# Feed-forward down stage: half rows kept in SBUF until their LayerNorm, the second half of the weight lookups split around the PSUM copies

## The chip, the core and the metric

The kernel runs on one NeuronCore of a Trainium2 chip. The metric is the device time of one execution in microseconds (us); lower is better. A core has TensorE (PE, matmuls into PSUM), VectorE (DVE), ScalarE (ACT), GpSimd (POOL) and SyncE (SP, which here issues all DMAs). Each engine works its own queue of instructions in order and waits on semaphores for the others.

## What is computed

One transformer block in float32 over 2048 rows of 1024: attention, and then a feed-forward part whose weights are 4-bit codes. Cut to what matters here:

```python
x = x + layernorm(attention(layernorm(x)))
# dequant(c, s) = NF4[c] * s, one scale per block of 64 inputs
h = layernorm(x)
inter = silu(h @ dequant(gate).T) * (h @ dequant(up).T)   # 2048 x 2752
y = inter @ dequant(down).T                               # 2048 x 1024
out = x + (y - mean(y)) / sqrt(var(y) + 1e-5)             # per row
```

The change lies in the last two lines: the down product and its LayerNorm with the residual.

## The kernel before

The stages follow each other on TensorE: projections and attention, output projection with LayerNorm, gate and up products, and from 2643 us on the down stage.

**Down stage, passes.** The 1024 output columns are taken in two halves (`n`), the 2048 rows in two groups (`g`) of eight tiles of 128 rows. That gives four passes (n, g) = (0,0), (0,1), (1,0), (1,1). In a pass the eight tiles accumulate in all eight PSUM banks, while `kt` runs over the 22 blocks of 128 inner columns (the last has 64). For each `kt`, `down` issues three matmuls per tile (a float32 number is split into two parts, `mm3`, L114 to L116; two matmuls at the last `kt`, L625 and L626). In the last pass alone the final six `kt` (LAST = 6) are held back and done tile by tile, so that the tiles are complete one after the other.

**Activations.** `load_inter` (L613, L616) brings 1 MB of `inter` per `kt` from HBM into a tile `it`, from the slot tag "hd", which has seven buffers of 8 KB per partition.

**Weights.** `down_weights` makes the weights of one (n, kt). `looked_up` loads the codes and scales into a tile `cs` (tag "pw", three buffers, L490 to L492), computes the NF4 value as minima and maxima of straight lines, seven lines `ln` on ACT (L499; tag "t2", three buffers) and ten operations on DVE (L494 to L512), and `split` writes the two parts into `wd` (L120, L121). Two `kt` share a buffer of `wd`, from the tags "pa", "w" and "xc" (13 buffers together, 11 needed for one half). So two pairs of the second half can be made at once, the others as pass (0,1) frees the buffers of the first half. `make(upto)` issues lookups in order until `upto` of the 44 are issued.

**Ends of passes.** With n = 0, `finish0` copies a bank to SBUF (L630; tile from "t2") and stores it to the HBM scratch `y0d` (L631). With n = 1, `finish1` reads that half back (L635), copies the other half from its bank (L636), loads the residual rows `xt` (L638; tag "pb", two buffers), takes the statistics (`ln_stats`, L126 to L134, a power on POOL at L132), and on DVE normalizes (L641) and adds (L642), half a row at a time, and stores to `out` (L643).

**Order.** The program is written with tile pools; a scheduler orders each engine's queue by the order in which the code issues work, by what is ready in its own timeline and by free buffers. A tile gets a buffer when one is free in the scheduler's order; the engines then keep that order on the chip.

The lines of the pass loop that the text speaks of:

```python
make(kt + 1 if (n, g) == (0, 0) else NIT + 4 + kt if (n, g) == (0, 1) else 2 * NIT)
it_ = load_inter(g, kt)
```

Of the kernel before, what the change touches and what calls it, by code (L numbers as in the profile page):

```python
# [10 lines left out]
F32 = mybir.dt.float32  # L11
# [3 lines left out]
AF = mybir.ActivationFunctionType  # L15
ALU = mybir.AluOpType
# [5 lines left out]
E = 1024  # L22
D = 64
I = 2752
P = 128
KE = E // P
NT = S // P
NC = S // 512
NIT = 22
# [28 lines left out]
def block_kernel(ctx, tc, x, wq, wk, wv, wo, gu_codes, gu_scales, d_codes, d_scales, cos_sin, out):  # L58
    nc = tc.nc
    V, A, G, T = nc.vector, nc.scalar, nc.gpsimd, nc.tensor  # L60
    load = nc.sync.dma_start
# [3 lines left out]
    dram = ctx.enter_context(tc.tile_pool(name="dram", bufs=1, space=DRAM))  # L65
# [8 lines left out]
    def slot(tag, shape, dtype, name):  # L74
        assert int(np.prod(shape[1:])) * 4 <= SLOTS[tag][1] * 1024, (tag, shape)
        return sb.tile(shape, dtype, tag=tag, name=name, bufs=SLOTS[tag][0])
# [6 lines left out]
    def any_bank():  # L83
        turn[0] += 1
        return bank(BANK_ORDER[turn[0] % 8])
# [37 lines left out]
    def ln_stats(row):  # L123
        st = small.tile([P, 2, 6], F32, tag="st", name="st")
        for i in range(2):
            V.bn_stats(st[:, i, :], row[i])  # L126
        mv = small.tile([P, 2], F32, tag="mv", name="mv")
        V.bn_aggr(mv, st.rearrange("p a b -> p (a b)"))
        ve = small.tile([P, 1], F32, tag="ve", name="ve")
        V.tensor_scalar(ve, mv[:, 1:2], EPS, None, ALU.add)  # L130
        rs = small.tile([P, 1], F32, tag="rs", name="rs")
        G.tensor_tensor(rs, ve, nhalf, ALU.pow)  # L132
        nb = small.tile([P, 1], F32, tag="nb", name="nb")
        V.tensor_scalar(nb, mv[:, 0:1], rs, -1.0, ALU.mult, ALU.mult)  # L134
        return mv[:, 0:1], rs, nb

    def halves(row):
        return row[:, :512], row[:, 512:]
# [19 lines left out]
    at = [dram.tile([E, 512], F32, tag=f"at{c}", name=f"at{c}") for c in range(NC)]  # L158
    x1d = dram.tile([S, E], F32, tag="x1d", name="x1d")
    ind = [[dram.tile([P, 2, 2, 512], F32, tag=f"ind{g}_{k}", name=f"ind{g}_{k}") for k in range(NIT)] for g in range(2)]  # L160
    y0d = [dram.tile([P, 512], F32, tag=f"y0d{t}", name=f"y0d{t}") for t in range(NT)]


    def prep_w(w, m, scale, tag="w"):
# [422 lines left out]
        ["pa", "xc"] + ["pa"] * 4 + ["w"] * 3 + ["pa", "xc"],  # L587
    )
    LAST = 6
    wd = {}  # L590

    def down_weights(n, kt):

        ns = slice(n * 512, (n + 1) * 512)
        if kt % 2 == 0:
            t = slot(WD_TAGS[n][kt // 2], [P, 2, 2, 512], FR, "wd")
            wd[n, kt], wd[n, kt + 1] = t[:, :, 0], t[:, :, 1]
        t = wd[n, kt]
        rows = P if kt < NIT - 1 else D
        b1 = min(2 * kt + 1, 42)  # L600
        m = looked_up(
            d_codes[kt * P : kt * P + rows, ns], d_scales[2 * kt : 2 * kt + 1, ns], d_scales[b1 : b1 + 1, ns], rows
        )
        if rows == P:
            split(t[:, 0], t[:, 1], m)
        else:
            A.copy(t[:, 0], m)
            V.tensor_tensor(t[D:, 0], m[D:], f32(t[D:, 0]), ALU.subtract)

    def load_inter(g, kt):  # L610
        t = slot("hd", [P, 2, 2, 512], FR, "it")
        if kt < NIT - 1:
            load(f32(t), ind[g][kt])  # L613
        else:
            for a in range(2):
                load(f32(t[a * D : (a + 1) * D]), ind[g][kt][:D])  # L616
        return t

    def down(o, it_, w, tt, first, last):

        i = it_[:, tt // 4, :, tt % 4 * P : (tt % 4 + 1) * P]
        if not last:
            mm3(o, i, w, first, False)
        else:
            T.matmul(o, lhsT=i[:, 0], rhs=w[:, 0], start=False, stop=False)  # L625
            T.matmul(o, lhsT=i[:, 1], rhs=w[:, 0], start=False, stop=True)  # L626

    def finish0(t, o):
        y0 = slot("t2", [P, 512], F32, "y0")
        A.copy(y0, o)  # L630
        load(y0d[t], y0)  # L631

    def finish1(t, o):
        y = slot("f4", [P, E], F32, "y")
        load(y[:, :512], y0d[t])  # L635
        A.copy(y[:, 512:], o)  # L636
        xt = slot("pb", [P, E], F32, "xt")
        load(xt, x1d[t * P : (t + 1) * P, :])  # L638
        mean, rs, _ = ln_stats(halves(y))
        for h in (slice(0, 512), slice(512, E)):  # L640
            V.tensor_scalar(y[:, h], y[:, h], mean, rs, ALU.subtract, ALU.mult)  # L641
            V.tensor_tensor(y[:, h], y[:, h], xt[:, h], ALU.add)  # L642
            load(out[t * P : (t + 1) * P, h], y[:, h])  # L643

    left = [(n, kt) for n in range(2) for kt in range(NIT)]

    def make(upto):
        while left and 2 * NIT - len(left) < upto:
            down_weights(*left.pop(0))

    for n in range(2):
        for g in range(2):
            os = [any_bank() for _ in range(8)]
            final = n == 1 and g == 1
            its = []
            for kt in range(NIT):

                make(kt + 1 if (n, g) == (0, 0) else NIT + 4 + kt if (n, g) == (0, 1) else 2 * NIT)
                it_ = load_inter(g, kt)
                if final and kt >= NIT - LAST:  # L660
                    its.append(it_)
                    continue
                for tt in range(8):
                    down(os[tt], it_, wd[n, kt], tt, kt == 0, kt == NIT - 1)
            for tt in range(8):
                for i, it_ in enumerate(its):
                    kt = NIT - LAST + i
                    down(os[tt], it_, wd[n, kt], tt, False, kt == NIT - 1)
                (finish0, finish1)[n](8 * g + tt, os[tt])


def _tables():
# [46 lines left out]
```

## Time and profile before

| what | value |
|---|---|
| time, median of 3 runs | 3166.28 us (3166.16 to 3166.58) |
| profiled execution: its time | 3171.26 us |
| profiled execution: its span, first to last instruction | 3169.5 us |
| mean granted TensorE clock | 0.976 |
| busy: PE / DVE / ACT / POOL | 95% / 69% / 57% / 22% of the span |
| down stage in the span | 2643 to 3169.5 us |

In the profile, PE is the matmul row and PEld the weight loads beside it. A group's row gives line, engine, operation, output<-input and count. A wait names the engine and line that waited, and after the arrow what released it. A timeline row has start, duration, engine, line, operation and, in brackets, the idle time before it with its releaser. "Landing" is the time from a DMA's issue to its data being there. Matmuls are pipelined: one takes 0.39 us, and the next starts 0.2268 us after it at the full clock.

### The profile page before, as it was taken

The numbers are of one execution on the slowest core, as the hardware profiler recorded it, in microseconds if no ns is written. First come the engines' busy times: TensorE is split into PE (matmuls) and PEld (weight loads), VectorE is DVE, ScalarE is ACT, GpSimd is POOL, SyncE is SP. The second block draws the span as 40 slices with busy tenths as digits, with TensorE's granted clock in tenths as the row PEclk, the third lists the DMA queues.
The fourth block names the chain that finished last, engine by engine and source line by source line (L and its number), as shares of the span: only waits on it lengthen the run. The fifth ranks groups of instructions, "written<-read, shape, count | busy, mean of one in ns | idle before, by whom it ended". The sixth has DMA issues, their size and how long they took to land.

```text
span 3169.5 us, 43461 instructions
## 1 busy us (share of the span) xinstructions
PE 3003.0 (95%) x14656; PEld 2471.0 (78%) x14656; DVE 2175.4 (69%) x4460; ACT 1813.5 (57%) x3822; POOL 700.2 (22%) x888
## 2 busy tenths in 40 slices
PE   7979999999999999989889999999999999995998
PEld 6868887787877777777667888888888888884886
DVE  7457777777867777776665986667766688498033
ACT  3246667676766666666555775556555567377000
POOL 4344444444443434453221000000000000000000
PEclk9989999999999999999989999999999999997999
DMA  8777666566637674743355332232222238885576
GB/s 313 246 232 228 207 208 198 175 190 178 202 131 197 194 224 155 223 135 114 110 193 172 121 113 92 94 107 100 90 96 94 100 115 281 261 271 190 206 293 228
DMA packets 251103, 560.70 MB, mean 177 GB/s; under 512 B 20736, under 2 KB 110848, under 8 KB 223744
## 3 DMA queue, kind: packets, MB, share of 16 engines
q1 hardware_dynamic: 250880, 557.93, 53.9%
q8 instruction: 116, 1.90, 0.2%
q14 instruction: 107, 0.88, 0.1%
HBM read 407.90 MB, written 149.95 MB: 176 GB/s over the span
## 4 chain that ended last, share of the span: by engine, by line
PE 77%; DMA 10%; DVE 6%; ACT 2%; POOL 2%; issue 2%; SPq 1%; DVEq 0%; POOLq 0%; ACTq 0%
PE bk L114 13%; PE bk L115 13%; PE bk L116 13%; PE pt L295 6%; PE qkv L114 5%; PE qkv L115 4%; PE qkv L116 4%; PE o L300 3%; PE s L256 3%; PE o L299 3%; PE s L258 3%; DMA wf<-in_wq 1%; DMA tab<-in_cos_sin 1%; DMA xc<-xd 1%; DMA cs<-in_d_codes 1%
## 5 line engine op out<-in xcount | busy, mean ns | idle before, releaser
L499 ACT ACTIVATE ln<-cs,bias 128x512 f32<-128x512 f32 x910 | 611.5, 717 | 132.5 <-DVE mp L505 39.3
L114 PE MATMUL bk<-x,wt 128*128 128x512 f32 x1376 | 535.9, 390 | 0.0
L115 PE MATMUL bk<-x,wt 128*128 128x512 f32 x1376 | 535.4, 389 | 0.0
L116 PE MATMUL bk<-x,wt 128*128 128x512 f32 x1376 | 535.1, 389 | 0.0
L285 POOL TENSOR_SCALAR prob<-prob,rc 128x512 f32<-128x512 f32 (+3 forms) x640 | 406.2, 655 | 408.4 <-DVE rc L280 260.1
L263 ACT ACTIVATE prob<-s,mxs 128x512 f32<-128x512 f32 (+3 forms) x640 | 400.8, 629 | 158.9 <-DVE mxs L262 144.6
L121 DVE TENSOR_TENSOR pw<-pt,pw 128x512 fp32r<-128x512 f32 (+3 forms) x640 | 377.1, 601 | 132.8 <-ACT pw L120 131.0
L262 DVE TENSOR_REDUCE mxs<-s 128x1 f32<-128x512 f32 (+3 forms) x640 | 379.5, 601 | 94.0 <-PE s L258 56.9
L120 ACT CAST pw<-pt 128x512 fp32r<-128x512 f32 (+3 forms) x640 | 322.8, 525 | 160.4 <-PE pt L295 132.7
L132 POOL TENSOR_TENSOR rs<-ve,nhalf 128x1 f32<-128x1 f32 x64 | 39.6, 638 | 1594.3 <-DVE ve L130 1588.3
L295 PE MATMUL pt<-ident,prob 128*128 128x128 f32 x2176 | 347.8, 276 | 3.3 <-DVE pw L121 3.0
L295 PEld LDWEIGHTS pt<-ident,prob 128*128 128x128 f32 x2176 | 268.0, 142 | 57.1 <-issue 4.2
L256 PE MATMUL s<-k,q 128*128 128x512 f32 (+3 forms) x640 | 268.2, 419 | 36.6 <-ACT prob L263 34.5
L114 PEld LDWEIGHTS bk<-x,wt 128*128 128x128 f32 x1376 | 258.7, 188 | 53.7
L115 PEld LDWEIGHTS bk<-x,wt 128*128 128x128 f32 x1376 | 258.5, 188 | 53.9
L116 PEld LDWEIGHTS bk<-x,wt 128*128 128x128 f32 x1376 | 258.4, 188 | 53.6
L114 PE MATMUL bk<-wd,it 128*128 128x512 f32 x672 | 261.9, 391 | 38.5 <-ACT y L630 38.5
L115 PE MATMUL bk<-wd,it 128*128 128x512 f32 x672 | 262.4, 390 | 0.0
L116 PE MATMUL bk<-wd,it 128*128 128x512 f32 x672 | 261.7, 390 | 0.0
L300 PE MATMUL o<-pw,v 128*128 128x512 f32 (+3 forms) x640 | 249.7, 392 | 4.3 <-DVE pw L121 4.0
L299 PE MATMUL o<-pw,v 128*128 128x512 f32 (+3 forms) x640 | 246.1, 385 | 7.6 <-ACT pw L120 7.0
L114 PE MATMUL qkv<-xc,w 128*128 128x512 f32 x576 | 235.7, 409 | 15.8 <-ACT w L174 10.1
(122 smaller groups left out, 5505.8 us busy)
## 6 DMA issues: line engine op xcount, KB each, us to landing
xc<-xd SPq DMA_DIRECT2D x96, 1024.0 KB, 9.0
it<-ind SPq DMA_DIRECT2D x84, 1024.0 KB, 7.7
ind<-hl SPq DMA_DIRECT2D x84, 512.0 KB, 2.6
q<-qs SPq DMA_DIRECT2D x128, 256.0 KB, 7.1
cs<-in_gu_scales SPq DMA_DIRECT2D x172, 128.0 KB, 3.0
cs<-in_gu_codes SPq DMA_DIRECT2D x86, 256.0 KB, 2.8
tab<-in_cos_sin SPq DMA_DIRECT2D x32, 512.0 KB, 10.5
xd<-xr SPq DMA_DIRECT2D x16, 1024.0 KB, 6.7
```

The costliest lines, as they stand in the source:

```text
L114: r = T.matmul(o, lhsT=w[:, 0], rhs=xx[:, 0], start=first, stop=False)
L115: T.matmul(o, lhsT=w[:, 0], rhs=xx[:, 1], start=False, stop=False)
L116: T.matmul(o, lhsT=w[:, 1], rhs=xx[:, 0], start=False, stop=last)
L121: V.tensor_tensor(lo, src, f32(hi), ALU.subtract)
L256: mm = T.matmul(s, lhsT=q[:, 0, j * P : (j + 1) * P], rhs=k[:, b:e], start=True, stop=False)
L262: V.tensor_reduce(mx, s, AX.X, ALU.max, negate=True)
L263: A.activation(prob[i][:, j, : e - b], s, AF.Exp, bias=mx, accum_out=sums[:, j % BATCH, i : i + 1])
L285: G.tensor_scalar(p, p, rc[:, jj % BATCH, i : i + 1], 0.0, ALU.mult, ALU.add)
L295: T.transpose(pt[:, j * P : (j + 1) * P], prob[kb // 4][:, j, kb % 4 * P : (kb % 4 + 1) * P], ident)
L299: T.matmul(o[:, cs], lhsT=v[:, kb, :], rhs=pw[:, 0, cs], start=kb == 0, stop=False)
L300: T.matmul(o[:, cs], lhsT=v[:, kb, :], rhs=pw[:, 1, cs], start=False, stop=kb == nk - 1)
L499: A.activation(ln, c8, AF.Identity, bias=bias_of[ab], scale=ab[0])
```

## The change

- The scratch `y0d` and the functions `finish0` and `finish1` go. `keep` copies a bank at the end of passes (0,0), (0,1) and (1,0) into a tile `kept` of four half rows: for n = 0 from the tag "hd" (four tiles, which share the seven buffers with `it`), for n = 1 from "xc" (two tiles).
- `finish` loads `xt`, takes the statistics of the two halves where they lie (in the last pass the right half is read in PSUM), turns `xt` into xt + nb on ACT (nb = -mean * rs, an Identity with a bias) and does half * rs + that on DVE in one multiply-add. For rows 0 to 7 all of it is issued after pass (1,0), for rows 8 to 15 in the last pass.
- In pass (0,1), lookups of the second half are issued only up to the first 16 (`SECOND`); the last six are issued after that pass's copies, with an edge that puts their ACT instructions behind the last copy.

```diff
-    y0d = [dram.tile([P, 512], F32, tag=f"y0d{t}", name=f"y0d{t}") for t in range(NT)]
...
+    SECOND = 16
...
-    def finish0(t, o):
-        y0 = slot("t2", [P, 512], F32, "y0")
-        A.copy(y0, o)
-        load(y0d[t], y0)
-
-    def finish1(t, o):
-        y = slot("f4", [P, E], F32, "y")
-        load(y[:, :512], y0d[t])
-        A.copy(y[:, 512:], o)
+    def keep(t, o, n):
+
+        if t % 4 == 0:
+            kept.setdefault(n, []).append(slot(("hd", "xc")[n], [P, 4, 512], F32, "kept"))
+        return A.copy(kept[n][t // 4][:, t % 4], o)
+
+    def finish(t, left, right):
+
         xt = slot("pb", [P, E], F32, "xt")
         load(xt, x1d[t * P : (t + 1) * P, :])
-        mean, rs, _ = ln_stats(halves(y))
-        for h in (slice(0, 512), slice(512, E)):
-            V.tensor_scalar(y[:, h], y[:, h], mean, rs, ALU.subtract, ALU.mult)
-            V.tensor_tensor(y[:, h], y[:, h], xt[:, h], ALU.add)
+        y = slot("f4", [P, E], F32, "y")
+        _, rs, nb = ln_stats((left, right))
+        for src, h in ((right, slice(512, E)), (left, slice(0, 512))):
+            A.activation(xt[:, h], xt[:, h], AF.Identity, bias=nb)
+            V.scalar_tensor_tensor(y[:, h], src, rs, xt[:, h], ALU.mult, ALU.add)
             load(out[t * P : (t + 1) * P, h], y[:, h])
...
-                make(kt + 1 if (n, g) == (0, 0) else NIT + 4 + kt if (n, g) == (0, 1) else 2 * NIT)
+                make(kt + 1 if (n, g) == (0, 0) else NIT + min(4 + kt, SECOND) if (n, g) == (0, 1) else 2 * NIT)
...
-                (finish0, finish1)[n](8 * g + tt, os[tt])
+                if final:
+                    finish(t, kept[0][t // 4][:, t % 4], os[tt])
+                else:
+                    last = keep(t, os[tt], n)
+            if (n, g) == (0, 1):
+                with tc.issue_after(last.ins):
+                    make(2 * NIT)
+            if (n, g) == (1, 0):
+                for t in range(8):
+                    finish(t, *(kept[i][t // 4][:, t % 4] for i in range(2)))
```

In the changed kernel the lines are: `it` loads L613 and L616, copies `keep` L632, load of `xt` L637, ACT lines of `finish` L641, multiply-adds L642, stores L643; lines of lookups stand one lower than before.

More of the change, by code (lines that the diff above doesn't have):

```diff
@@ L626, in down @@
             T.matmul(o, lhsT=i[:, 1], rhs=w[:, 0], start=False, stop=True)
-    def finish0(t, o):
-        y0 = slot("t2", [P, 512], F32, "y0")
-        A.copy(y0, o)
-        load(y0d[t], y0)
-    def finish1(t, o):
-        y = slot("f4", [P, E], F32, "y")
-        load(y[:, :512], y0d[t])
-        A.copy(y[:, 512:], o)
+    def keep(t, o, n):
[3 more added lines that the diff above has]
+    def finish(t, left, right):
         xt = slot("pb", [P, E], F32, "xt")
         load(xt, x1d[t * P : (t + 1) * P, :])
-        mean, rs, _ = ln_stats(halves(y))
-        for h in (slice(0, 512), slice(512, E)):
-            V.tensor_scalar(y[:, h], y[:, h], mean, rs, ALU.subtract, ALU.mult)
-            V.tensor_tensor(y[:, h], y[:, h], xt[:, h], ALU.add)
+        y = slot("f4", [P, E], F32, "y")
[3 more added lines that the diff above has]
+            V.scalar_tensor_tensor(y[:, h], src, rs, xt[:, h], ALU.mult, ALU.add)
             load(out[t * P : (t + 1) * P, h], y[:, h])
+    kept = {}
     left = [(n, kt) for n in range(2) for kt in range(NIT)]
@@ L665, in block_kernel @@
             for tt in range(8):
+                t = 8 * g + tt
                 for i, it_ in enumerate(its):
```

## Prediction

> **What bounds the kernel now.** I read the busy slices first, then the waits from 2643 us on (where the down stage starts on TensorE), then timelines of the places that they name. In the slices, PE stands at 9 nearly everywhere, with one hole, a 5 in slice 37 (2852 to 2932 us).
>
> ```profile
> PE   7979999999999999989889999999999999995998
> ...
> PEclk9989999999999999999989999999999999997999
> ```
>
> The waits of the down stage (who waited for whom: us in total, times, longest) say what the hole is: one wait of PE for ACT's PSUM copy (L630).
>
> ```profile
> DVE mp L504 <- ACT ln L499: 44.7, 1, 44.7
> ...
> PE bk L114 <- ACT y L630: 38.5, 1, 38.5
> DVE st L126 <- DMA y<-y0d: 33.3, 9, 14.2
> ACT y L630 <- PE bk L626: 31.3, 1, 31.3
> ```
>
> The timelines of ACT and PE show why. The bank is complete at about 2876, but ACT works its queue in order, and the lookups of the second half of the weights stand in front of the copy:
>
> ```profile
> 2757.47 0.39 PE L625 MATMUL bk<-wd,it 128*128 128x512 f32 x1
> 2758.18 1.57 ACT L630 COPY y<-bk 128x512 f32<-128x512 f32 x3 [31.34 <-PE bk L626]
> ...
> 2878.73 0.39 PE L626 MATMUL bk<-wd,it 128*128 128x512 f32 x1
> ...
> 2917.00 1.21 ACT L630 COPY y<-bk 128x512 f32<-128x512 f32 x2
> 2917.62 0.80 PE L114 MATMUL bk<-wd,it 128*128 128x512 f32 x1 [38.50 <-ACT y L630]
> ```
>
> The lookups are late because at the end of the first pass it is the other way round: ACT sits in front of eight copies (31.3 us), so DVE does nothing for 44.7 us. Call the passes 00, 01, 10, 11 (weight half, row half). A pass is 520 matmuls 0.2268 us apart, 117.9 us. Measured: 00 ends at 2761.1, 01 at 2879.0, the wait ends at 2917.6, 10 at 3038.3 (120.7 long, 2.8 over), 11 at 3156.3, and 13.2 us later the span ends.
>
> The 2.8 us are the clock, in the stretches of 20 us (columns: us; PE, PEld, DVE, ACT, POOL busy; clock; DMA):
>
> ```profile
> 2880.00:2900.00 20.00, 0.00 (x0) 0.00 (x0) 17.89 (x33) 15.57 (x24) 0.00 (x0) 0.56 0.56 183
> 2900.00:2920.00 20.00, 2.38 (x6) 1.90 (x7) 19.09 (x34) 15.31 (x24) 0.00 (x0) 0.50 0.26 84
> 2920.00:2940.00 20.00, 20.00 (x83) 16.36 (x82) 2.29 (x4) 3.35 (x6) 0.00 (x0) 0.92 0.57 205
> ```
>
> Last, how long transfers take. First the `it` loads (1 MB) in four stretches: burst of four at 2607, beside lookups (2780 to 2870), alone (2940 to 3030), beside LN traffic (3060 to 3100); then the `xt` loads (512 KB) at the end (3138 to 3160).
>
> ```profile
> DMA to landing us min/median/max: 4.9/10.3/13.5
> DMA to landing us min/median/max: 6.2/8.1/10.6
> DMA to landing us min/median/max: 4.5/4.8/6.2
> DMA to landing us min/median/max: 6.1/10.2/14.3
> DMA to landing us min/median/max: 4.2/5.2/5.6
> ```
>
> **The change, part by part.** I put the two built programs' instruction order side by side. Up to the last lookups of the first weight half (about 2720 us) every engine has the same order, so all differences lie in the down stage.
>
> *The hole between 01 and 10: minus 41.4.* At most 16 of the 22 lookups of the second half now stand ahead of 01's copies; the other six stand behind. They also start earlier, since no `y0` copy blocks the `ln` buffers: about six are done before 00 ends. A lookup takes 6.3 us (casts to `wd` at 2889.25 and 2895.48). Lookups 4 to 15 wait for weight buffers that 01 frees (pair k of the first half, 10.7 us each; the last is freed after kt 11, at about 2830), so number 15 is done by about 2840, ahead of 01's end. Gone: 38.6 of wait and 2.8 of clock. The six behind take 38 us and are needed at kt 16, 86 us into pass 10: nothing. They are covered by that pass; without it they would cost their 38.
>
> *A new wait between 00 and 01: plus 4.0, and clock 1.7.* (a) On ACT, lines of lookups 0 to 6 now precede the first copy. DVE has about 63 instructions from 2722.84 to the one that frees the last `ln` buffer among them; at 6.28/11 = 0.57 us each that is 2759.5, a line 0.72, first copy done at 2761: just in time. (b) On SP, the five `it` loads of pass 01 used to go out from 2730.5 on; now the two `kept` tiles take the first two freed "hd" buffers, and the loads are issued after the code loads of lookup 7, which need a `cs` buffer that DVE's multiply of lookup 4 frees, at 2757.7. Three issues later, about 2760, the first `it` goes out; the first of the burst of four landed in 4.9, so PE starts at 2765 instead of 2761.1. Bounds: 0 (DVE a lookup faster than I count) and 9 (lookups at 7 us and a landing of 8.1). The next loads land 3 us apart ((13.5-4.9)/3), faster than PE's 5.4 per kt.
>
> Clock after this wait: the only row is the 38.5 us gap, which cost 2.8. [...] By the row alone I could say anything from 0 to 2.8[...]. No short gap is shown here; I take 1.7. [...]
>
> *Copies at the other boundaries: plus 0.3.* The eight `keep` copies (0.59 each) are spread over banks that complete 0.45 apart, as before; PE needs bank i 0.68 after bank i-1.
>
> *`it` buffers, 7 down to 5, then 3 in pass 10.* A buffer freed by kt k must be filled again for kt k+3, 10.7 us later. Alone the loads land in 4.8, beside lookups in 8.1: nothing. In pass 11 they land in 10.2 beside LN traffic. That stretch also held eight `y0d` reads of 256 KB, which go; the remaining 1 MB per row (load and stores) is spaced out by SP's order, about one row between two `it` loads. I take 0; bounds 0 and 8.
>
> *End of pass 11: plus 2.7.* The last six `it` tiles are held together (LAST), but two of seven "hd" buffers still hold `kept` rows. So the built order puts kt 21 of all eight banks at the very end: its load waits until bank 7 has used kt 16. Then 12 matmuls are left (2.7 us), against about 0.2 wait, 0.5 for the first of two issues and 4.7 to land (alone): 5.4, PE idle 2.7. Bounds 1.5 and 5.
>
> *The tail: 13.2 becomes 33.3, plus 20.1.* Before, banks complete 3.85 us apart and rows are finished as they come. Now all banks complete within 3.2 us, the first at T = end - 3.2, and eight rows come at once. In DVE's order 12 stats (0.61 each) and about a dozen small ones (1.3 in all) precede the first multiply-adds: rows 8 and 9 done at T+10.2 and T+11.7. Rows 10 to 15 need `xt`, and there are two buffers: the load for row r+2 is issued when row r's second multiply-add is done and its stores are issued (0.45), lands (4.6; least 4.0, median 5.2 shown), then two ACT lines (1.33; nearest row L499, 0.72, starts 0.6 apart), and the second multiply-add (0.65), 0.2 of hand-over: 7.25 per pair of rows, three times 21.8. Row 15 is done at T+33.5, and the last store lands 3.0 later (before: last add ends at 3166.5, span 3169.5): T+36.5 is 33.3 after PE. [...]
>
> *LN as ACT line and one multiply-add.* DVE loses a TENSOR_SCALAR per half row (0.45 to the next start), 0.9 per row; ACT gets two lines per row (1.3) and, in rows 8 to 15, loses the copy (0.59). Multiply-adds from PSUM: nearest is the reduction from PSUM (L262, 601 ns), no dearer than from SBUF. In pass 11 this is hidden under PE; in the tail it is in the sum above. The `y0d` stores and reads (32 issues, 8.4 MB) go: nothing on the path but the 33.3 us for which the stats waited for them, hidden or in the 13.2.
>
> **Sum**: -41.4 + 5.7 + 0.3 + 2.7 + 20.1 = -12.6. Against the profiled execution (3171.26; its span 3169.5) that is 3158.7; the median of the runs is 5.0 below that execution, so 3166.28 - 12.6 = 3153.7. No change, for this kernel, is within 0.2%, 6.3 us.
>
> **The rivals.** *A. Nearly the whole gain:* the first `it` load is in time at the end of 00[...]: -41.4 + 0.3 + 2.7 + 15.9 = -22.5, 3143.8. For it: two estimates with little slack; against: the measured `xt`. 13%.
>
> *B. Gain given back in the tail:* in the tail of before, rows two apart ended 11.5 us apart (adds ended at 3144.2 and 3155.7, 3148.7 and 3160.1), although the reads of `y0d` were in that. At 11 us a pair, the tail is 8.5 + 33 + 3 = 44.5, the sum -1.4, 3164.9: no change. 13%.
>
> *C. Slower: three `it` buffers starve PE.* In passes 10 and 11 PE gets three kt per (landing + 0.3 + 5.4). From a mean landing of 10.4 that is over 5.36 a kt; over 34 kt the gain is gone at 11.5 and 0.2% is lost at 12.1. At 12.5: 0.71 x 34 = 24 more, 3177.8. For it: 10.2 with up to 14.3 in pass 11; against: 4.8 in pass 10. 6%.
>
> That lookups don't reorder as said is excluded by the built order.
>
> **How the numbers follow.** My own case 68%: 3153.7; nearly all of it is faster by over 0.2% (66 of 68; 2 no change). With A 13, faster is 79%. No change is B and part of mine, with 1 lost to C's side: 14%. Slower 7%. Range: 3141 (A with a little more) to 3166 (B); C and the edges, under 2 in 10, are left out.
>
> **What would show it.** Right: no PE wait at 2879, pass 10 at 117.9; a wait of 3 to 6 for `it` near 2761; 2 to 4 for `it` before the last 16 matmuls; after PE's end, L642 in pairs 7 us apart waiting for L641, that for DMA xt<-x1d. Wrong: PE waiting for `it` within passes (C), pairs at 11 (B), an end 25 us after PE (A), or a copy L632 behind lookups by more than 4 us at 2761.

## The result, and the profile after

The changed kernel takes 3161.18 us (median of 20 runs, 3157.52 to 3176.39), the kernel before, run beside it, 3162.78 us (20 runs, 3157.18 to 3167.0). The ratio, formed from all these runs and not from the two medians (which alone would give 0.9995), is 1.0002, 95% interval 0.9992 to 1.0011. On another occasion the same two programs gave 0.9989 (0.9981 to 0.9997; 22 and 30 runs). So it is no change, or a gain of up to about 0.2%, 6 us; 0.4% was forecast. The time lies in the stated range, the likeliest case was not the one that came.

Much of the spread between runs comes from the stages that the change doesn't touch: in the twelve profiles of this study the first matmul of the down stage begins anywhere between 2631.7 and 2645.2 us. So from here on the down stage is measured by itself, from its first matmul to the end of the span. It was 526.3 us in the first profile of the kernel before and is 520.3 us in the profile of the changed one. The page of the changed kernel, the rows of PE and its granted clock:

```profile
PE   7979999999999999989889999999999999999995
...
PEclk9989999999999999999989999999999999999997
```

The hole in slice 37 is gone; the last slice is now a 5. The waits from 2643 us on:

```profile
ACT xt L641 <- DMA xt<-x1d: 45.5, 12, 9.0
DVE y L642 <- ACT xt L641: 33.8, 12, 6.1
...
PE bk L114 <- ACT kept L632: 6.6, 1, 6.6
PE bk L625 <- DMA it<-ind: 4.3, 1, 4.3
```

In place of one wait of 38.5 PE has two short ones, and ACT and DVE have a new chain with `xt` in it. The timeline of PE shows where the two are, and that both are followed by slow matmuls (0.77 for the first, instead of 0.39):

```profile
2758.37 0.39 PE L626 MATMUL bk<-wd,it 128*128 128x512 f32 x1
2765.32 0.77 PE L114 MATMUL bk<-wd,it 128*128 128x512 f32 x1 [6.56 <-ACT kept L632]
...
3122.37 0.77 PE L625 MATMUL bk<-wd,it 128*128 128x512 f32 x1 [4.34 <-DMA it<-ind]
...
3127.32 0.39 PE L626 MATMUL bk<-wd,it 128*128 128x512 f32 x1
```

PE ends at 3127.7, 28.6 us earlier than before (26.1 if both are counted from the first down matmul); the span ends at 3161.0, 33.3 us after PE. The stretches around the ends of pass 00 (2758) and pass 01, with the clock in the column after POOL:

```profile
2760.00:2780.00 20.00, 14.69 (x54) 12.01 (x55) 14.55 (x25) 12.71 (x23) 0.00 (x0) 0.83 1.01 365
2860.00:2880.00 20.00, 20.00 (x89) 16.55 (x89) 0.00 (x0) 0.00 (x0) 0.00 (x0) 1.00 0.32 86
2880.00:2900.00 20.00, 20.00 (x90) 16.57 (x89) 12.24 (x22) 16.31 (x27) 0.00 (x0) 1.00 0.64 218
```

At the end of pass 01 PE doesn't stop, and DVE and ACT are idle before it: the 16 lookups have long been done.

### The profile page after: what moved, and what is told of

It reads as the page before. It is cut to its first block, busy times and chain, and to the rows that moved or that the text cites. A ratio compares the mean times of both kernels' runs of the same rounds, so it can differ in the third digit from the quotient of the medians.

```text
span 3161.0 us, 43388 instructions
## 1 busy us (share of the span) xinstructions
PE 3007.8 (95%) x14656; PEld 2474.5 (78%) x14656; DVE 2161.6 (68%) x4428; ACT 1827.9 (58%) x3846; POOL 700.3 (22%) x888
## 4 chain that ended last, share of the span: by engine, by line
PE 79%; DMA 9%; DVE 6%; ACT 2%; issue 1%; SPq 1%; POOL 1%; DVEq 0%; ACTq 0%; POOLq 0%
PE bk L114 13%; PE bk L115 13%; PE bk L116 13%; PE pt L294 6%; PE qkv L114 5%; PE qkv L116 5%; PE qkv L115 5%; PE o L299 3%; PE s L255 3%; PE o L298 3%; PE s L257 3%; DMA wf<-in_wq 1%; DMA xc<-xd 1%; DMA cs<-in_d_codes 1%; PE pj L440 1%
## 5 line engine op out<-in xcount | busy, mean ns | idle before, releaser
L255 PE MATMUL s<-k,q 128*128 128x512 f32 (+3 forms) x640 | 268.1, 419 | 35.2 <-ACT prob L262 33.5
```

Source lines behind the costliest of these rows:

```text
L255: mm = T.matmul(s, lhsT=q[:, 0, j * P : (j + 1) * P], rhs=k[:, b:e], start=True, stop=False)
```

## The experiments

In this table "stage" is from the first down matmul to the span's end, "PE" from there to the end of the last matmul, "tail" the rest; all three from the one profile of each run, in us, each rounded by itself. The ratio is that of the timed runs to the kernel before on the same occasion.

| kernel | stage | PE | tail | ratio (95%) |
|---|---|---|---|---|
| before, first profile | 526.3 | 513.1 | 13.2 | |
| before, again | 521.8 | 508.7 | 13.1 | 0.9994 (0.9982 to 1.0005) |
| changed, first profile | 520.3 | 487.0 | 33.3 | 1.0002 (0.9992 to 1.0011) |
| changed, again | 519.7 | 487.2 | 32.5 | 0.9989 (0.9981 to 0.9997) |
| e1 LAST = 5 | 499.8 | 482.4 | 17.3 | 0.9918 (0.9904 to 0.9931) |
| e2 five `xt` buffers | 512.7 | 489.4 | 23.3 | 0.9965 (0.9952 to 0.9979) |
| e3 lookups behind pass 00's copies | 511.6 | 478.8 | 32.9 | 0.9968 (0.9955 to 0.9981) |
| e4 before + split alone | 486.6 | 473.8 | 12.9 | 0.9872 (0.9854 to 0.9890) |
| e5 changed, no split | 519.4 | 486.7 | 32.7 | 0.9986 (0.9976 to 0.9995) |
| e6 e1 + e2 + e3 | 480.8 | 471.6 | 9.2 | 0.9868 (0.9851 to 0.9886) |
| e7 changed, LN of before | 519.8 | 486.2 | 33.6 | 0.9988 (0.9979 to 0.9997) |
| e8 e4 + five `xt` buffers | 484.0 | 472.1 | 11.9 | 0.9874 (0.9857 to 0.9891) |

**The two kernels once more.** No edit.

> The changed kernel once more, for a second profile and a second ratio. Theory (gain given back): the same picture as in the first profile: no wait at the end of pass 01, about 7 us at the end of pass 00, about 4.5 us before the last 16 matmuls, 33 us from PE's end to the end of the span, down stage 520 us; 0 to 7 us under the kernel before, ratio 0.998 to 1.000. Rival (the first profile was a lucky or unlucky one): one of these places is off by more than 3 us.

> The kernel before once more, for a second profile of it. Theory: the same as in the first profile: one wait of 38 to 39 us at the end of pass 01, tail 13 us, down stage 525 to 527 us, so that the changed kernel's stage (520.3 and 519.7) is really 6 shorter and the rest of the difference between runs comes from the stages before. Rival: the wait or the tail varies from run to run, and the stage is 520 to 522 here, as long as the changed one.

The changed kernel showed the same places again; this time the first wait is put down to the load, not to the copy. The load is what ends it in the first profile too: the first `it` load, issued at 2758.2, landed 7.0 later, at 2765.2, and PE starts 0.1 after that, at 2765.32, while the first copy was done at 2761.1. In the four other profiles with this wait (e1, e2, e5, e7; 5.6 to 8.9 us) it is put down to the load as well.

```profile
PE bk L114 <- DMA it<-ind: 6.4, 1, 6.4
PE bk L625 <- DMA it<-ind: 4.4, 1, 4.4
```

The kernel before had the same wait for ACT, but 35.2 us long and not 38.5:

```profile
PE bk L114 <- ACT y L630: 35.2, 1, 35.2
```

So the expectation of an unvarying stage failed, and the rival's came true: the stage is 4.5 us shorter than in the first profile, 3.3 of it in the wait and 1.1 in the slow restart after it (1.7 lost instead of 2.8). The stage of the changed kernel is 1.5 to 6.6 us shorter than that of the kernel before, by the profiles that one pairs; of the two ratios the first allows at most 2.5 us, the second 1 to 6.

**e1: the last six held tiles become five.**

```diff
-    LAST = 6
+    LAST = 5
```

> LAST = 5 in place of 6: five tiles held together fit in the five free buffers, so the last kt needn't wait and banks complete one after the other, 3.2 us apart. Theory: the wait before the last 16 matmuls (4.5 and 1.8 of clock) goes, and rows are finished as banks complete, in two chains of 7 us a pair: tail about 9 us in place of 33. Together 27 to 31 us under the changed kernel, ratio to before about 0.991. Rival (the tail is bound by xt loads whatever the banks do): only the 6 us of the wait go, tail stays over 28, ratio about 0.998.

The wait before the last matmuls is gone, and the tail is 17.3. The stage is 20 us shorter, not 27 to 31: PE gained 4.5 (the 6.0 of the wait and its restart, less a first wait that was 2 us longer here, though with a cheaper restart), and the tail is 8 us longer than expected. One reason is that only the last banks complete 3.2 us apart. The first three complete together, at 3102.8, 3103.3 and 3103.7, 16 us before PE's end, and DVE has nothing to do until then:

```profile
3102.85 1.30 DVE L126 BATCH_NORM_STATS2 st<-bk 128x6 f32<-128x512 f32 x2 [57.84 <-PE bk L626]
```

Then the stats of three rows and more stand ahead of the first multiply-add, so the two chains start at 3107.8, 11 us before PE's end, and run at 7 us a pair. That the tail depends on when the banks complete is clear; the rival's 28 is not seen.

**e2: more buffers for `xt`.**

```diff
-        xt = slot("pb", [P, E], F32, "xt")
+        xt = slot("pb" if t < 8 or (t - 8) % 5 < 2 else "pw", [P, E], F32, "xt")
```

> Five buffers for the residual rows in the last pass in place of two (three of the idle tag pw besides), nothing else. Theory (the tail is the chain load of xt, ACT line, multiply-add, with two buffers): tail 33 down to about 21 us, 10 to 13 us under the changed kernel; PE up to its end as before, with the 4.5 us wait. Rival (the tail is DVE's work on eight rows at once, 12 stats and 16 multiply-adds): tail stays within 3 us of 33.

The tail fell from 33 to 23.3, and rows 10 to 13 now end 1.5 us apart on DVE:

```profile
3143.01 0.74 DVE L642 SCALAR_TENSOR_TENSOR y<-bk,rs,xt 128x512 f32<-128x512 f32 x1
3143.67 0.74 DVE L642 SCALAR_TENSOR_TENSOR y<-kept,rs,xt 128x512 f32<-128x512 f32 x1
3144.46 0.74 DVE L642 SCALAR_TENSOR_TENSOR y<-bk,rs,xt 128x512 f32<-128x512 f32 x1
3145.24 0.74 DVE L642 SCALAR_TENSOR_TENSOR y<-kept,rs,xt 128x512 f32<-128x512 f32 x1
...
3149.34 0.75 DVE L642 SCALAR_TENSOR_TENSOR y<-bk,rs,xt 128x512 f32<-128x512 f32 x1 [1.80 <-DMA out<-y]
```

The two buffers held the tail, 10 us of it. Two us more than expected remain, since the last two rows wait for the stores that free their `y` buffers (four). The stage is only 7.0 to 7.6 us shorter, since PE took 2.2 to 2.4 longer: the first wait was 8.9 in this profile.

**e3: all but four lookups behind the copies of pass 00.**

```diff
-                make(... NIT + min(4 + kt, SECOND) if (n, g) == (0, 1) else 2 * NIT)
+                if (n, g) == (0, 1):
+                    make(NIT + 4)
+                    with tc.issue_after(last.ins):
+                        make(NIT + min(4 + kt, SECOND))
```

> In pass 01 all lookups of the second half but the first four get the edge that puts their ACT lines behind the last copy of pass 00 (the same form of edge as the change uses at the end of pass 01); in the built order 28 lines fewer... of lookups precede the copies (four lookups, not six and a half) and two code loads fewer precede the five it loads. Theory: the 7 us wait and its 2.5 us of clock at the end of pass 00 go, at most 2 us left: 7 to 9 us under the changed kernel. Rival (the wait is the 7 us landing of a 1 MB load that starts late because of the kept buffers, not of the lookups ahead of it): the wait stays at 5 to 7 us.

(By the built order it is 17 lines fewer that precede the copies; of the code loads one fewer, not two, precedes the first `it` load.) The wait is gone altogether; the stage is 8 to 9 us shorter. ACT stood waiting for the banks:

```profile
2752.51 4.01 ACT L632 COPY kept<-bk 128x512 f32<-128x512 f32 x8 [4.42 <-PE bk L626]
```

And SP, in the timeline of its queue, issued the first `it` load at 2749 and not at 2758, 6.0 us earlier if both are counted from the first down matmul:

```profile
2749.08 12.35 SPq L613 DMA_DIRECT2D it<-ind  x6
```

**e4: the split alone, in the kernel before.**

```diff
-                make(... NIT + 4 + kt if (n, g) == (0, 1) else 2 * NIT)
+                make(... NIT + min(4 + kt, SECOND) if (n, g) == (0, 1) else 2 * NIT)
...
-                (finish0, finish1)[n](8 * g + tt, os[tt])
+                last = (finish0, finish1)[n](8 * g + tt, os[tt])
+            if (n, g) == (0, 1):
+                with tc.issue_after(last.ins):
+                    make(2 * NIT)
```

(`finish0` returns its copy.) 

> One part of the change alone, in the kernel before: the limit of 16 lookups ahead of pass 01's copies and the edge for the last six; halves still go through y0d, seven it buffers, LN as before. Theory: the split alone takes the whole wait (38.5 and 2.8 of clock) or all but 5 of it, and nothing is paid back, since the it buffers and the order of the last pass stay: stage 485 to 491, tail 13 to 15, ratio 0.987 to 0.989. Rival (the lookups must start before the end of pass 00, as only the kept tiles allow): 16 lookups from 2771 on end at 2877 at the earliest, a wait of 10 or more remains, ratio over 0.991.

One wait is left in PE's down stage (L631 is this kernel's copy of a bank to `y0`), and no payment:

```profile
PE bk L114 <- ACT y L631: 1.4, 1, 1.4
```

The stage is 35 to 40 us shorter than before, 1.3% of the time. The split by itself is worth nearly the whole hole. The rival had the lookups right, but not the wait: the 16th is done at 2881.4, but the first copy goes ahead of its last ACT instruction, at 2877.2. The 1.4 us that is left is for a copy at 2888.2, which itself waited for stores of earlier copies to `y0d`.

**e5: the changed kernel without the split.**

```diff
-    SECOND = 16
+    SECOND = 22
```

> The changed kernel without the split: all 22 lookups of the second half stand ahead of pass 01's copies (SECOND = 22), halves kept in SBUF. Theory (it is the earlier start, six lookups done before pass 00 ends, that matters as much as the split): the last lookup ends at about the end of pass 01, a wait of 0 to 4 us there, time within 4 us of the changed kernel. Rival (the split is what removes the wait): a wait of 25 us or more comes back, ratio about 1.008.

Nothing changes; ACT is done with the last lookup at 2868.4 and waits for the banks:

```profile
2867.80 0.62 ACT L607 CAST wd<-mp 128x512 fp32r<-128x512 f32 x1 [2.71 <-DVE mp L511]
2873.43 4.01 ACT L632 COPY kept<-bk 128x512 f32<-128x512 f32 x8 [5.01 <-PE bk L626]
```

So the hole can be closed in two ways, and the change has both: start the lookups before pass 00 ends, or put six of them behind the copies. With one the other is idle. In the changed kernel it is the earlier start that does it, and the split adds nothing.

**e6: the three repairs together** (edits of e1, e2, e3).

> The changed kernel with three repairs: LAST = 5, five buffers for the residual rows of the last pass, and all but four lookups of the second half behind pass 00's copies. Theory (the three payments are separate): no wait over 2 us in the down stage, PE's matmuls 473 to 476, tail 9 to 13 us; stage 484 to 489, ratio 0.986 to 0.989. Rival (they overlap: the tail only moves into DVE or the loads of it): tail over 16, ratio over 0.990.

PE has no wait for another engine or a transfer in this stage, and the tail is 9.2. The stage is 480.8, under the 484 to 489 expected. The three payments are separate, and they are all of what was paid: PE's part, 471.6, is about four passes of 117.9.

**e7: the LayerNorm of before in the changed kernel.**

```diff
-        _, rs, nb = ln_stats((left, right))
+        mean, rs, _ = ln_stats((left, right))
...
-            A.activation(xt[:, h], xt[:, h], AF.Identity, bias=nb)
-            V.scalar_tensor_tensor(y[:, h], src, rs, xt[:, h], ALU.mult, ALU.add)
+            V.tensor_scalar(y[:, h], src, mean, rs, ALU.subtract, ALU.mult)
+            V.tensor_tensor(y[:, h], y[:, h], xt[:, h], ALU.add)
```

> The changed kernel with the LayerNorm of before on DVE: subtract and multiply, then add, in place of the ACT line and one multiply-add. Theory (the tail is the chain of two xt buffers, and the ACT lines stand in that chain): after a load only two adds are left (1.3 us in place of 2.2), so the tail is 2 to 3 us shorter, 30 to 31, although DVE has 0.9 us more per row; time 0 to 4 us under the changed kernel. Rival (DVE bounds the tail, so taking work off it helped): the tail is 4 to 7 us longer, 37 to 40.

Both were wrong: the tail is 33.6, as with the new form. Its adds in the timeline:

```profile
3133.88 1.29 DVE L642 TENSOR_TENSOR y<-y,xt 128x512 f32<-128x512 f32 x2
...
3153.55 1.29 DVE L642 TENSOR_TENSOR y<-y,xt 128x512 f32<-128x512 f32 x2 [2.43 <-DMA xt<-x1d]
```

Row 9 ends at 3135.2, 10.9 us after PE's end (3124.2), against 7.6 with the new form, since the subtractions of later rows stand ahead on DVE. From there to row 15 it takes 19.7 us, 6.6 a pair, against 22.8 and 7.6. The chain is shorter by an ACT line, and starts later by about as much. The new form of LN neither gains nor costs here.

**e8: the split alone with five `xt` buffers** (e4 with the edit of e2).

> The kernel before with the split alone, and five buffers for the residual rows of the last pass. Theory: PE as with the split alone (474 us to PE's end), tail down from 12.9 to the last row's own work, copy 0.6, stats and small ones 2.2, two and two DVE operations 2.2, last store 3: 8 to 9 us; 4 us under the split alone, ratio to before 0.985 to 0.987. Rival (the reads of y0d bound that tail): stays at 12 to 13.

The tail fell by 1.0 only, to 11.9, and the ratio is that of e4. The chain of work that ended last shows what comes ahead of PE's end (3110.0) here: a store that frees a `y` buffer, and then the read of `y0d` into that buffer (start, duration, what):

```profile
3102.66 3.63 DMA out<-y
...
3106.35 2.66 DMA y<-y0d
```

From its landing at 3109.0 DVE works through the last three rows until 3118.9 with one wait over 0.2 us (0.73, for POOL), and the last store follows. So the reads that the rival names stand in the chain, together with the stores ahead of them; it was not tried whether the tail shrinks without them. e4 and e6 are the best kernels here, 1.3% under the kernel before, and not to be told apart by their intervals. e4 needs a quarter of the changed lines (11 of 43).

## Why the prediction came out as it did

In the first profiles of both kernels, term by term:

| step | predicted | measured |
|---|---|---|
| hole after pass 01 and its clock | -41.4 | -41.4 (38.66 + 2.76) |
| wait after pass 00 and its clock | +5.7 | +9.2 (6.7 + 2.5) |
| copies at the other ends of passes | +0.3 | 0 |
| wait for the last kt, its clock | +2.7 | +6.0 (4.5 + 1.5) |
| tail, 13.2 to 33.3 | +20.1 | +20.1 |
| sum | -12.6 | -6.1 (stage: -6.0) |

**Right.** Every place was named, with its cause: e4 and e5 show the hole's, e3 the wait after pass 00, e1 the one at the end, e2 the tail. The tail's chain, told as 7.25 us per pair of rows, took 7.6 from row 9 to row 15. That the tail's sum fits to 0.1 us is luck: row 9 was done 0.9 us sooner after PE's end than worked out (7.6 instead of 8.5), and the three pairs took 1.0 longer; the second profiles give +19.4. Rival C didn't come: no wait for `it` within a pass, with medians of 4.8 for landings alone and 9.0 beside LN traffic (12.6 the longest), where it begins at a mean of 10.4. Rival B, no change, came about by another way; its 11 us a pair were not seen. A's early load was not seen either; its 15.9 for the tail rested on an estimate of how soon `xt` lands that no run had shown (4.2 to 5.6 us was at hand; the six loads of the changed tail took 3.7 to 5.4). The hole was credited to the split as well as to the earlier start, but by the prediction's own figures (lookup 15 done at 2840, 6.3 us each) all 22 would have been done at 2878, ahead of the pass's end; in e5 they are, with 8 us to spare.

**Wrong: the sizes of the two new waits and of their restarts.** Worked out were 5.7 and 2.7, together 8.4; measured were 9.2 and 6.0, together 15.2, and 15.4 in the second profile. First, "the first of the burst of four landed in 4.9, so PE starts at 2765". The load was issued at 2758.2 (the stage began 2.5 us earlier in this profile, so that is 2760.7 by the prediction's clock, 0.7 after the estimate), but five loads went out within 2.3 us, and the first, which was the quickest, took 7.0:

```profile
L613 SPq DMA_DIRECT2D it<-ind x5: 368/522/1013, 2758.2 to 2760.5; - x5
...
DMA to landing us min/median/max: 7.0/10.9/15.8
```

The prediction's second row, 6.2 to 10.6 beside lookups, was at hand and was taken only as a bound. The copies, worked out as "just in time", were late too: the first was done at 2761.1, 2.4 us after the pass's end, which the later landing hides.

Second, the wait for the last kt: 4.5 where 2.7 was worked out. The last kt is loaded in two pieces, and 4.7 to land was taken for the second. The last two loads of the changed kernel:

```profile
DMA to landing us min/median/max: 4.6/5.5/6.4
```

The second piece took 6.4, which is 1.7 more and nearly all of the error; in the kernel before it took 6.4 as well. A slow restart followed, 1.5 us, which I had set at nothing.

Third, the clock. The 1.7 for the restart after the first wait was my estimate alone: the one row at hand, a wait of 38.5 us that cost 2.8, left anything from 0 to 2.8 open, and no short wait had been shown. Measured in this profile: after the first wait twelve starts in a row came about 0.43 us apart instead of 0.227, 2.5 us lost (in the second profile 1.6; more on this below). The two waits with their clocks are 3.5 and 3.3 us over; the 0.3 of the other copies was not needed, which leaves 6.5, the error of the sum in the table.

**Wrong: what it was measured against.** The term of the hole was read from one execution, a wait of 38.5. In a second it is 35.2. And the sum was taken from 3166.28, the median of three runs, where twenty give 3162.78. The difference of a single pair of profiles, 6 us, was therefore partly the luck of the first one; the two ratios leave 0 to 6. That the measured time lies in the range has luck in it as well: the upper end was put where B would have come out, and B did not come.

None of this is a failed mechanism, but a forecast of 79% for a gain over 0.2% gave the sum of five terms, each with an error of 1 to 4 us, too much trust. My bounds for the first wait (0 and 9) and the last (1.5 and 5) held both measured waits at their upper parts, and the upper bounds with the restarts that were measured (2.5 and 1.5) come close to nothing: -41.4 + 11.5 + 0.3 + 6.5 + 20.1 is -3.0, no change.

## What to carry to other kernels

When a queue in program order holds work for later in front of a copy that frees PSUM, move the queue's order, alone, and look at what is left (here 1.3%). Buffers that are borrowed to save a trip through HBM are paid for where their owner needed them: here in the order in which banks complete (e1). Work that starts earlier can in turn stand ahead of a load that is needed sooner (e3). And a change with several parts wants each part run alone: the split alone gains nearly everything; the tiles kept in SBUF close the same hole without it, but what comes with them gives the gain back in three other places; LN does nothing that shows.

## What the runs showed of the hardware

In the down stages of the twelve profiles TensorE has fourteen waits of 4.4 us or more, and after each it restarted at about half rate. After seven of them 7 or 8 starts in a row came about 0.44 us apart instead of 0.227, which lost 1.5 to 1.8 us; after the other seven it was 12 or 13 starts, and 2.5 to 2.8 us. The length of the wait does not decide which: 38.7 us cost 2.8, but 35.3, the same wait in the second profile of the kernel before, cost 1.7; at the end of the changed kernel 4.5 us cost 1.5 in one profile and 4.6 cost 2.6 in the other. The stretches of 10 us from the restart in the two profiles of the kernel before (the clock after POOL):

```profile
2917.00:2927.00 10.00, 9.38 (x30) 7.48 (x31) 4.50 (x7) 5.09 (x10) 0.00 (x0) 0.68 0.75 260
2909.00:2919.00 10.00, 9.43 (x35) 7.66 (x36) 4.41 (x7) 5.04 (x10) 0.00 (x0) 0.80 0.77 258
```

What decides is not shown. A wait of 4 to 7 us cost a quarter to six tenths more than its length here; the wait of 1.4 us in e4 cost 0.1 more.

Five loads of 1 MB issued within 2.3 us landed between 7.0 and 15.8 us after their issue (first profile of the changed kernel), against 4.8, the median for loads with nothing beside them in the kernel before. The first of the five, too, took 7.0, while the first of the four at 2607 in the kernel before, issued 1.4 us apart, landed in 4.9. Whether the closer issue did it or the code loads issued just ahead, no run separates.

The last tile of 1 MB, loaded as two pieces of 64 partitions issued 0.5 us apart, was complete 6.9 us after the first issue in the first profiles of both kernels (the first piece took 4.7 and 4.6, the second 6.4 in both), against 4.8, the median, for a tile of the same size loaded at once.
